# A 3x3 convolution with a second transform: columns as well as rows, and a running sum that lives in the output

## The chip, the cores and the metric

The kernel runs on one core of one Trainium2 chip. The metric is the device time of one execution in microseconds (us). A core has five engines that run side by side and meet through semaphores: PE (TensorE, matrix products), DVE (VectorE), ACT (ScalarE), POOL (GpSimd, here an issuer of DMAs) and SP (SyncE, an issuer of DMAs). PE's weight loads are listed apart as PEld. All DMAs run on the same 16 DMA engines.

## The reference

Four layers work on an input of 4 images x 256 channels x 64 x 64 pixels, fp32. Each adds to its input a function of the group-normalised input. Only the last one is changed; the others deliver its input in three pieces.

```
x = x + attention(gn(x))        # layer 0
x = x + ternary_conv(gn(x))     # layer 1
x = x + binary_block(gn(x))     # layer 2
x = x + conv3x3(gn(x), W) + bias  # layer 3: 256 -> 256 channels, 3x3, padding 1
...
W = weight * a / (1 + exp(weight * b))   # built from 64 x 64 x 3 x 3 and 16 pairs a, b
gn(v): mean and variance over 8 channels x 64 x 64 pixels of one image
```

## The kernel before, in words

The 256 channels are two tiles of 128 partitions, named t as an input (0 or 1) and co as an output. An image has 4096 pixels, which layer 3 handles in two halves h of 32 rows. A chunk is one image b, one half h and one output tile co: 16 chunks in all.

**The transform of layer 3.** The convolution's 3 rows of taps are replaced by a transform over rows (Winograd F(4,3)): six input rows give six transformed rows v[k], and six products m[k] give four output rows. Columns are plain: each v[k] is multiplied by three weight matrices, one for each dx, on windows of 64 columns shifted by dx. So a chunk has 6 (k) x 2 (t) x 3 (dx) = 36 products of 128x128 weights with 8 x 64 = 512 columns, all fp32 (line 1078). The weights are made in layer 0's score stage by the generator `weights_3`, a few DVE instructions at each step, and wait in DRAM (`u3_d`).

**`conv_layer`** holds layer 3. `prepare(b, t)` calls `load_3`: it loads x2 (layer 2's input), z and, for t=0, y (layer 2's output) and sums them in SBUF with scales that batch normalisation gave (`sg`, `sy2`): lines 1748, 1755 and 1758. The halves of the sum have six fixed buffers x0 to x5, by the table `X_PLACES`. Statistics come from `bn_stats` on DVE (line 1126), for the very first tile from ACT squares (line 1761). `norm` turns them into a scale and a shift, with small matmuls (lines 115 to 128). `transform(b, t, h)` writes the normalised half with ACT into a padded buffer (lines 1194 and 1198) and calls `input_rows`, 12 DVE instructions (lines 1052 to 1065), into one of six buffers t0 to t5. `chunk` calls `output_rows`: the products, two ACT copies (line 1096), 14 DVE instructions (lines 1098 to 1113), of which the last four add the result onto the sum in SBUF. `finish_3` stores that to `out` with one DMA of 1 MB from POOL (line 1772).

**Order.** `rest()` gives the program order; a list scheduler of the framework places the instructions of each engine by priority and expected time, and each engine then runs its own list strictly in that order. `high_priority` and `keep_in_program_order` override it in places. Products go into a ring of seven PSUM banks. For the first chunk, all products of t=1 are issued ahead of those of t=0 (`order = (1, 0)`), so that PE can begin before t=0 is ready.

**The border.** Layer 2 ends with convolutions of image 3. Its buffers and layer 3's share SBUF: a pool of layer 3 lies over what layer 2 has there, and each of its tiles waits until that is read. Of the sum, x and z are ready early; the scale `sy2` of y needs the statistics of all of layer 2.

Of the kernel before, what the change touches and what calls it, by code (L numbers as in the profile page):

```python
# [9 lines left out]
F32 = mybir.dt.float32  # L10
# [8 lines left out]
P = 128  # L19
B = 4  # L20
# [21 lines left out]
def network(ctx: ExitStack, tc, x, wqkv, relm, relt, relw, relv, counts, masks, vecs, rowv, ab, w1, l2w1, l2w2, l3w, mats, out):  # L42
# [25 lines left out]
    u3_d = scratch("u3_d", [P, 2, 3, 6, C])  # L68
    bk_d = [dram.tile([P, 2, 3, 4 * 3 * 64], BF16, name=f"bk_d{i}", tag=f"bk_d{i}") for i in range(2)]
# [339 lines left out]
    with ExitStack() as ph:  # L409
# [161 lines left out]

        def weights_2(i, g):
# [28 lines left out]
        def weight_steps():  # L601
            for t in range(2):
                for dx in range(3):
                    yield from weights_3(t, dx)
                    yield
            for i in range(2):
                for g in range(2):
                    yield from weights_2(i, g)
                    yield
# [137 lines left out]
    def from_scores(general, keep):  # L747
# [300 lines left out]
        def input_rows(v, pad, pinned):  # L1048

            d = [pad[:, r : r + 29 : 4, :] for r in range(6)]  # L1050
            stt = nc.vector.scalar_tensor_tensor
            start = stt(v[:, 5], d[2], -4.0, d[4], ALU.mult, ALU.add)
            if pinned:
                tc.keep_in_program_order(start)
            stt(v[:, 0], d[1], -4.0, d[3], ALU.mult, ALU.add)
            nc.vector.tensor_tensor(v[:, 1], v[:, 5], v[:, 0], ALU.add)  # L1056
            nc.vector.tensor_tensor(v[:, 2], v[:, 5], v[:, 0], ALU.subtract)
            nc.vector.tensor_tensor(v[:, 5], d[4], d[2], ALU.subtract)
            nc.vector.tensor_tensor(v[:, 0], d[3], d[1], ALU.subtract)
            stt(v[:, 3], v[:, 0], 2.0, v[:, 5], ALU.mult, ALU.add)  # L1060
            stt(v[:, 4], v[:, 0], -2.0, v[:, 5], ALU.mult, ALU.add)
            stt(v[:, 0], d[0], 4.0, d[4], ALU.mult, ALU.add)
            stt(v[:, 0], d[2], -5.0, v[:, 0], ALU.mult, ALU.add)
            stt(v[:, 5], d[1], 4.0, d[5], ALU.mult, ALU.add)
            stt(v[:, 5], d[3], -5.0, v[:, 5], ALU.mult, ALU.add)

        def output_rows(ring, taken, op, u, vs, co, xh, bias, name, order):


            ms = [None] * 6  # L1070
            c, sm = [None, None], [None, None]

            def product(k, t, first, last):
                if first:
                    ms[k] = ring[taken[0] % len(ring)].tile([P, 8, 64], F32, name=f"{name}_{k}", tag="conv")
                    taken[0] += 1
                for dx in range(3):
                    nc.tensor.matmul(  # L1078
                        ms[k], lhsT=u[t][:, dx, k, bass.ts(co, P)], rhs=vs[t][:, k, :, dx : dx + 64],
                        start=(first and dx == 0), stop=(last and dx == 2),  # L1080
                    )

            if order:
                for k in range(6):
                    product(k, order[0], True, False)
            for k in range(6):
                if order:
                    product(k, order[1], False, True)
                else:
                    product(k, 0, True, False)  # L1090
                    product(k, 1, False, True)
                if k in (2, 4):
                    i = k // 2 - 1
                    c[i] = op.tile([P, 8, 64], F32, name=f"{name}_c{i}", tag=f"c{i}", bufs=1)
                    sm[i] = op.tile([P, 8, 64], F32, name=f"{name}_s{i}", tag=f"s{i}", bufs=1)
                    nc.scalar.copy(c[i], ms[k])  # L1096
                    if i == 0:
                        nc.vector.scalar_tensor_tensor(sm[i], ms[1], bias, c[i], ALU.add, ALU.add)
                        nc.vector.scalar_tensor_tensor(c[i], ms[1], bias, c[i], ALU.add, ALU.subtract)
                    else:  # L1100
                        nc.vector.tensor_tensor(sm[i], ms[3], c[i], ALU.add)
                        nc.vector.tensor_tensor(c[i], ms[3], c[i], ALU.subtract)
            x4 = xh.rearrange("p (q r w) -> p q r w", r=4, w=64)
            (d12, d34), (s12, s34) = c, sm
            o = [op.tile([P, 8, 64], F32, name=f"{name}_o{r}", tag="o", bufs=1 if general else 2) for r in range(4)]
            nc.vector.tensor_tensor(o[0], ms[0], s12, ALU.add)
            nc.vector.tensor_tensor(o[0], o[0], s34, ALU.add)
            nc.vector.scalar_tensor_tensor(o[1], d34, 2.0, d12, ALU.mult, ALU.add)
            nc.vector.scalar_tensor_tensor(o[2], s34, 4.0, s12, ALU.mult, ALU.add)
            nc.vector.scalar_tensor_tensor(o[3], d34, 8.0, d12, ALU.mult, ALU.add)  # L1110
            nc.vector.tensor_tensor(o[3], ms[5], o[3], ALU.add)
            for r in range(4):
                nc.vector.tensor_tensor(x4[:, :, r, :], x4[:, :, r, :], o[r], ALU.add)
# [16 lines left out]
        X_PLACES = [(0, 1, 2, 3), (4, 5, 0, 2), (1, 3, 4, 0), (5, 2, 1, 4)]  # L1130

        def conv_layer(name, ph, weights, layout, own, load, biases, first, finish):
# [3 lines left out]
            ps_ = {k: pool(ph, f"{name}_{k}", 2 if k in ("a", "o") else 1) for k in layout.split()}  # L1136
            ap_, op, sp = ps_["a"], ps_["o"], ps_["s"]
            pst = pool(ph, f"{name}_pst", 1, PSUM)
            ring = [pool(ph, f"{name}_ps", 7, PSUM)]
# [3 lines left out]
            u = [ps_[f"u{t}"].tile([P, 3, 6, C], F32, name=f"{name}_u{t}", tag="u") for t in range(2)]  # L1143

            def set_up():
                for h in range(2):
                    nc.vector.memset(pads[h][:, 33 * h, :], 0.0)
                    nc.vector.memset(pads[h][:, 1 - h : 34 - h, 0], 0.0)
                    nc.vector.memset(pads[h][:, 1 - h : 34 - h, 65], 0.0)

            def load_weights(t, eng):
                for dx in range(3):
                    eng.dma_start(out=u[t][:, dx], in_=weights[:, t, dx])

            xs, vs, mvs, shifts = {}, {}, {}, {}

            def place(b, t):
                xs[b, t] = []
                for h in range(2):
                    s = X_PLACES[b][2 * t + h]  # L1160
                    xs[b, t].append(ps_[f"x{s}"].tile([P, HW // 2], F32, name=f"{name}x_{b}_{t}_{h}", tag="x"))
                return xs[b, t]

            def prepare(b, t):
                if t == 0 or b not in mvs:
                    mvs[b] = small(sp, [P, 2, 2])
                st = sp.tile([P, NB, 6], F32, name=f"{name}st_{b}_{t}", tag=f"st{t}")
                shifts[b, t], done = load(b, t, place(b, t), ap_, st, mvs[b][:, t, :], sp, pst, pads[0])
                if not done:
                    nc.vector.bn_aggr(mvs[b][:, t, :], st.rearrange("p k s -> p (k s)"))  # L1170
                if shifts[b, t] is not None:
                    nc.vector.tensor_tensor(mvs[b][:, t, 0:1], mvs[b][:, t, 0:1], shifts[b, t], ALU.add)

            norms = {}

            def norm(b, ts):
                gm, rs = norm_stats(sp, pst, mvs[b], ts, own, name)
                for t in range(ts.start, ts.stop):
                    i = t - ts.start
                    nb = small(sp, [P, 1])  # L1180
                    if shifts[b, t] is None:
                        nc.vector.scalar_tensor_tensor(
                            nb, gm[:, i : i + 1], -1.0, rs[:, i : i + 1], ALU.mult, ALU.mult
                        )
                    else:
                        nc.vector.tensor_tensor(nb, shifts[b, t], gm[:, i : i + 1], ALU.subtract)
                        nc.vector.tensor_tensor(nb, nb, rs[:, i : i + 1], ALU.mult)
                    norms[b, t] = nb, rs[:, i : i + 1]

            def transform(b, t, h, pinned=False):  # L1190

                nb, rs = norms[b, t]
                own_, other = xs[b, t][h], xs[b, t][1 - h]
                nc.scalar.activation(
                    pads[h][:, 1:33, 1:65], own_.rearrange("p (h w) -> p h w", w=64), AF.Identity, bias=nb, scale=rs
                )
                row_, dst = (other[:, 0:64], 33) if h == 0 else (other[:, HW // 2 - 64 : HW // 2], 0)
                nc.scalar.activation(pads[h][:, dst, 1:65], row_, AF.Identity, bias=nb, scale=rs)
                s = 2 * ((2 * b + h) % 3) + t
                v = ps_[f"t{s}"].tile([P, 6, 8, 66], F32, name=f"{name}tr_{b}_{t}_{h}", tag="tr")  # L1200
                input_rows(v, pads[h], pinned)
# [12 lines left out]
            def rest():  # L1214
                for b in range(B):
                    chunk(b, 0, 0, first if b == 0 else None)
                    if b + 1 < B:
                        prepare(b + 1, 0)
# [690 lines left out]
```

## Time and profile before

| | us |
|---|---|
| three runs | 2726.46, 2732.78, 2739.72 |
| median | 2732.78 |
| the profiled execution, own time | 2720.99 |
| span in its profile | 2719.2 |
| PE busy | 2391.5 (88%) |
| DVE busy | 1976.9 (73%) |
| ACT busy | 1204.6 (44%) |
| POOL busy | 104.7 (4%) |
| line 1078, the products of layer 3 | 503.7 |

The span runs from the first to the last instruction of the profiled execution; its own time is 1.8 us longer. Busy shares are averages over stages with different limits, so what matters for layer 3 is its own stage, the last 540 us. An idle time in a row stands before the group's own instructions, with what ended it.

### The profile page before, as it was taken

Reading aid. Unit: us, or ns where it says so; the run is one execution under the profiler, and the core shown is the slowest. Engines: PE = TensorE matmul, PEld = TensorE weight load, DVE = VectorE, ACT = ScalarE, POOL = GpSimd, SP = SyncE. Lnnn points to the kernel's source line nnn. Section 1 sums busy time; section 2 is a strip of 40 time slices with the busy share of each in tenths; the row PEclk is TensorE's granted clock in tenths of the full one; section 3 lists DMA queues with packets and bytes.
Section 4 is the critical chain, followed back from the end, with each engine's and each line's share of the span. In section 5 each row is a group of like instructions: output and inputs, shape, how many; then the busy total and the mean of one; then the engine's idle time right before and its main releaser. Section 6 shows DMA issues by size and latency. Waiting matters only on the chain. (4 is left out here: it accounts for less than half of the span.)

```text
span 2719.2 us, 78126 instructions
## 1 busy us (share of the span) xinstructions
PE 2391.5 (88%) x34632; PEld 1578.0 (58%) x34632; DVE 1976.9 (73%) x3370; ACT 1204.6 (44%) x1986; POOL 104.7 (4%) x201
## 2 busy tenths in 40 slices
PE   7999888888997788889775999998979869999998
PEld 4666655656665666667664777775545424444443
DVE  6766789888765465666668989887888877867742
ACT  4556355555555544454445666553458311110100
POOL 0000100000001000000000000000000000000000
PEclk9999899999999898988986999999989979999999
DMA  6866466666666877777777656424347742424110
GB/s 240 259 195 196 129 192 172 167 171 183 154 149 164 263 265 239 262 239 255 254 230 268 205 165 200 163 94 163 127 156 256 270 155 102 145 93 139 47 47 32
DMA packets 287996, 489.87 MB, mean 180 GB/s; under 512 B 32736, under 2 KB 149088, under 8 KB 274848
## 3 DMA queue, kind: packets, MB, share of 16 engines
q1 hardware_dynamic: 224992, 359.52, 43.5%
q0 software_dynamic: 14400, 66.53, 6.3%
q10 hardware_dynamic: 48256, 58.73, 6.3%
q8 instruction: 273, 4.47, 0.7%
q14 instruction: 75, 0.61, 0.1%
HBM read 281.46 MB, written 203.23 MB: 178 GB/s over the span
## 5 line engine op out<-in xcount | busy, mean ns | idle before, releaser
L1078 PE MATMUL gc<-gtr,g_u 128*128 128x512 f32 x1152 | 503.7, 599 | 12.0 <-DVE gtr L1056 6.7
L1078 PEld LDWEIGHTS gc<-gtr,g_u 128*128 128x128 f32 x1152 | 220.1, 192 | 287.5 <-issue 269.4
L515 DVE STREAM_TRANSPOSE t<-pd 128x1024 f32<-128x1024 f32 x256 | 304.4, 1228 | 86.1 <-PE pd L508 85.2
L508 PE MATMUL pd<-rm,qb 64*32 64x256 f32 x8192 | 307.2, 392 | 41.4 <-DVE t L515 32.3
L1469 PE MATMUL pc<-e_tr,e_k 128*64 128x512 bf16 x2304 | 264.8, 391 | 18.8 <-DVE e_tr L1458 11.7
L535 ACT ACTIVATE o<-pq 128x512 f32<-128x512 f32 x256 | 150.2, 592 | 270.2 <-PE pq L529 265.9
L1365 PE MATMUL dc<-dh,d_u 128*128 128x512 f32 x768 | 230.5, 411 | 20.9 <-ACT dh L1342 20.2
L508 PEld LDWEIGHTS pd<-rm,qb 64*32 64x32 f32 x8192 | 170.8, 109 | 133.2 <-DVE t L515 58.9
L919 ACT ACTIVATE pt<-pt,sm 128x512 f32<-128x512 f32 x256 | 162.3, 709 | 174.8 <-DVE pt L889 174.8
L1365 PE MATMUL dc<-dl,d_u 128*128 128x512 f32 x768 | 227.5, 407 | 2.5 <-DVE dl L1343 2.4
L1469 PEld LDWEIGHTS <-e_k 128*64 128x64 bf16 x2304 | 147.1, 113 | 133.4 <-issue 26.6
L529 PEld LDWEIGHTS pq<-t,t 64*64 64x64 f32 x8192 | 144.5, 137 | 84.7 <-issue 73.5
L529 PE MATMUL pq<-t,t 64*64 64x64 f32 x8192 | 166.9, 224 | 26.7 <-issue 22.2
L1365 PEld LDWEIGHTS dc<-dh,d_u 128*128 128x128 f32 x768 | 146.9, 193 | 61.4 <-ACT dh L1342 21.6
L1096 ACT COPY gc_c<-gc 128x512 f32<-128x512 f32 x32 | 18.6, 580 | 344.3 <-PE gc L1078 344.3
L1365 PEld LDWEIGHTS dc<-dl,d_u 128*128 128x128 f32 x768 | 145.6, 191 | 43.6 <-DVE dl L1343 5.2
L889 DVE TENSOR_TENSOR pt<-e_False,si_False 128x1024 f32<-128x1024 f32 x123 | 145.7, 1215 | 26.9 <-PE e_False L877 26.7
L877 PE MATMUL e_False<-qc_False,rw 32*128 32x256 f32 x984 | 128.4, 481 | 28.1 <-DVE pt L889 13.0
L541 ACT ACTIVATE sq<-o 128x1024 bf16<-128x1024 f32 x128 | 135.3, 1057 | 3.9
L291 PE MATMUL po<-xg,wt 128*128 128x512 f32 x256 | 120.3, 610 | 7.6 <-DVE st L298 6.0
L982 PE MATMUL pe_False<-pt,ve 128*32 128x64 f32 x4096 | 91.1, 243 | 36.9 <-issue 31.3
L957 PE MATMUL pa_False<-pt,vb 128*32 128x64 f32 x4096 | 100.0, 242 | 25.1 <-DVE o_False L966 18.1
(404 smaller groups left out, 3645.9 us busy)
## 6 DMA issues: line engine op xcount, KB each, us to landing
si_False<-qk_d SPq DMA_DIRECT2D x64, 1024.0 KB
qk_d<-o SPq DMA_DIRECT2D x496, 128.0 KB
x<-x_d SPq DMA_DIRECT2D x32, 1056.0 KB
xa<-in_x SPq DMA_DIRECT2D x16, 1024.0 KB
vt_d<-vs ACTq DMA_DIRECT2D x32, 512.0 KB
q_d<-qs SPq DMA_DIRECT2D x64, 256.0 KB
qb<-q_d SPq DMA_DIRECT2D x128, 128.0 KB
qc_False<-q_d SPq DMA_DIRECT2D x64, 256.0 KB
```

Source lines behind the costliest of these rows:

```text
L291: nc.tensor.matmul(psf, lhsT=wt[:, t, bass.ts(o, P)], rhs=xg[:, t, :], start=(t == 0), stop=(t == 1))
L508: nc.tensor.matmul(pds[t][32 * c : 32 * c + 32, m].rearrange("p j k -> p (j k)"), lhsT=q[rows, 2 * (gp % 2) + g, a, 32 * nb : 32 * nb + 32 ...
L515: nc.vector.transpose(ts[t][:, :, 32 * jh : 32 * jh + 32].rearrange("p a j b -> p j a b"), pds[t].rearrange("p m j k -> p j m k"),)
L529: nc.tensor.matmul(ps[nb][64 * g : 64 * g + 64, m, :], lhsT=ts[1][rows, n // 2, :, n % 2], rhs=ts[0][rows, n // 2, :, n % 2], start=True, ...
L535: nc.scalar.activation(o[:, :, n : n + 8, :], ps[nb].rearrange("p n (a b) -> p a n b", b=2), AF.Copy, accum_out=acc[:, nb, gp, col : col + 1],
L541: nc.scalar.activation(junk, part, AF.Square, accum_out=acc[:, 2, gp, col : col + 1])
L877: nc.tensor.matmul(rows_of_e[x_][:, :, :, par], lhsT=rw[rows, 63 - i : 127 - i].rearrange("p j r -> p (j r)"), rhs=q[rows, :, par, k % 2, ...
L889: nc.vector.tensor_tensor(dst, e, src, ALU.add)
L919: nc.scalar.activation(s, s, AF.Exp, scale=s2q[:, gp : gp + 1])
L1078: nc.tensor.matmul(ms[k], lhsT=u[t][:, dx, k, bass.ts(co, P)], rhs=vs[t][:, k, :, dx : dx + 64], start=(first and dx == 0), stop=(last and ...
L1365: nc.tensor.matmul(at[k], lhsT=u[t][:, dx, k, bass.ts(co, P)], rhs=v[:, k, :, dx : dx + 64], start=(first and p_ == 0 and dx == 0), stop=( ...
L1469: nc.tensor.matmul(m[64 * g : 64 * g + 64], lhsT=parts[:, g, i, k, dx, :], rhs=vs[g][:, k, 8 * (q % 2) : 8 * (q % 2) + 8, dx : dx + 64], s ...
```

## The change

- **Columns.** Products of even k (0, 2, 4) get a second transform over columns (Winograd F(2,3)): `input_columns` makes from four shifted column sets, with a step of two elements, four sets of 32 columns, and four weight matrices replace three. Each is a product with 8 x 32 = 256 columns. Two of the four share a PSUM bank as its halves. Odd k stay as they were. A chunk has 18 products of 512 columns and 24 of 256.
- **Weights.** `weights_c` makes the two mixed column weights from `u3_d` and stores them in `uc_d`. `load_weights` takes six DMAs for each t.
- **Output.** `columns` (two ACT half copies and one DVE sum from PSUM) and `whole` (one DVE sum that interleaves the columns) undo the column transform. The sum is not added on DVE: the result `o4` is added onto `out` in DRAM by a POOL DMA with `accum_op`. Only image 3's h=1 adds on DVE and stores from SP, in two parts. `o4` has one buffer.
- **Inputs.** `load_3` sums pieces of 512 pixels in rings: x five deep, z four, y three. Each sum is stored to `out` from ACT's queue; its statistics come from DVE's accumulated sum and an ACT square. `fetch` reads 33 rows back from `out` (POOL queue) for `transform`. Image 0's first half stays in SBUF, its x and z are asked for early, and its y comes as one DMA into the place of the t=0 weights.
- **Buffers and order.** Transformed inputs have four places for six; t=1 goes ahead with seven of the nine tiles; loads of the next image are held until a transform is done (`issue_after`). Layer 2's y tiles get a pool for each image.

```diff
+        def weights_c(t):
+            nc.gpsimd.dma_start(out=a, in_=u3_d[:, t, 0, 0:6:2])
+            nc.gpsimd.dma_start(out=c, in_=u3_d[:, t, 2, 0:6:2])
+            nc.gpsimd.dma_start(out=u[:, 3:6], in_=u3_d[:, t, 1, 0:6:2])
...
+            pinned(v.tensor_tensor(c, a, c, ALU.add))
+            v.tensor_scalar(c, c, 0.5, None, ALU.mult)
+            pinned(v.scalar_tensor_tensor(u[:, 0:3], u[:, 3:6], 0.5, c, ALU.mult, ALU.add))
+            v.scalar_tensor_tensor(u[:, 3:6], u[:, 3:6], -0.5, c, ALU.mult, ALU.add)
+            nc.gpsimd.dma_start(out=uc_d[:, t].rearrange("p c k o -> p (c k) o"), in_=u)
...
+        def input_columns(w, v):
+            f = v.rearrange("p k q w -> p (k q) w")
+            d = [f[:, :, r : r + 63 : 2] for r in range(4)]
+            for c, (i, j, op) in enumerate(
+                ((0, 2, ALU.subtract), (1, 2, ALU.add), (2, 1, ALU.subtract), (3, 1, ALU.subtract))
+            ):
+                last = nc.vector.tensor_tensor(w[:, c].rearrange("p k q w -> p (k q) w"), d[i], d[j], op)
+            return last
+
+        TILES = [(1, None), (2, (1, 2)), (2, (0, 3)), (3, None), (4, (1, 2)), (4, (0, 3)), (0, (1, 2)), (0, (0, 3)), (5, None)]
...
+                    for a, c in enumerate(cs):
+                        nc.tensor.matmul(
+                            m[:, a], lhsT=u2[:, c, k // 2, bass.ts(co, P)],
+                            rhs=v2[:, c, k // 2].rearrange("p q w -> p (q w)"), start=first and a == 0, stop=last and a == 1,
+                        )
...
+            def columns(i, copied, scratch_):
+                pair = halves(flat(ms[i]))
+                c2 = halves(copied)
+                nc.scalar.copy(c2[:, 0], pair[:, 1])
+                nc.scalar.mul(c2[:, 1], pair[:, 1], -1.0)
+                sd = halves(scratch_)
+                nc.vector.tensor_tensor(sd, pair[:, 0:1].to_broadcast([P, 2, 256]), c2, ALU.add)
+                return sd
+
+            def whole(i, sd, dst):
+                nc.vector.tensor_tensor(
+                    dst.rearrange("p (n a) -> p a n", a=2), halves(flat(ms[i])), sd, ALU.add
+                )
...
+            if res is None:
+                nc.gpsimd.dma_start(out=out_, in_=of, accum_op=ALU.add)
+            else:
+                for half in range(2):
+                    cols = bass.ts(half, HW // 4)
+                    nc.vector.tensor_tensor(of[:, cols], of[:, cols], res[:, cols], ALU.add)
+                    nc.sync.dma_start(out=out_[:, cols], in_=of[:, cols])
...
+            ps_ = {k: pool(ph, f"{name}_{k}", {"x": 5, "z": 4, "y": 3}.get(k, 1)) for k in layout.split()}
...
+            def fetch(b, t, h):
+                raws[b, t, h] = raw(b, t)
+                nc.gpsimd.dma_start(
+                    out=raws[b, t, h].rearrange("p q w -> p (q w)"),
+                    in_=out[b, bass.ts(t, P), 31 * h * 64 : (31 * h + 33) * 64],
+                )
...
                     chunk(b, 0, 0, first if b == 0 else None)
-                    if b + 1 < B:
-                        prepare(b + 1, 0)
+                    if more:
+                        with tc.issue_after(ready[b, 0, 0]):
+                            prepare(b + 1, 1)
                     chunk(b, 0, 1, None)
-                    if b + 1 < B:
-                        prepare(b + 1, 1)
+                    if more:
+                        with tc.issue_after(ready[b, 0, 1]):
+                            prepare(b + 1, 0)
                         norm(b + 1, slice(0, 2))
+                        for t in range(2):
+                            fetch(b + 1, t, 0)
                     chunk(b, 1, 0, None)
-                    if b + 1 < B:
+                    if more:
                         for t in range(2):
                             transform(b + 1, t, 0)
+                            fetch(b + 1, t, 1)
...
-            yp = pool(ph, "e_y")
+            yps = {b: pool(ph, f"e_y{b}") for b in (3, 0, 1, 2)}
...
+                    nc.scalar.activation(a, xt, AF.Square, accum_out=st[:, k, 1:2])
+                    if raw is None or k > 3:
+                        nc.scalar.dma_start(out=dst[:, bass.ts(k, HW // 8)], in_=xt)
...
+                if later:
+                    with tc.issue_after(loaded[0]):
+                        nc.sync.dma_start(out=y0, in_=y_d[0])
```

## The prediction

> **What bounds the kernel now.** I read the page's groups first, then stages, then time lines of PE and DVE across the border of the last two layers. The change touches only the last convolution, from about 2130 us, so that stage decides.
>
> ```profile
> L1078 PE MATMUL gc<-gtr,g_u 128*128 128x512 f32 x1152 | 503.7, 599 | 12.0 <-DVE gtr L1056 6.7
> L1078 PEld LDWEIGHTS gc<-gtr,g_u 128*128 128x128 f32 x1152 | 220.1, 192 | 287.5 <-issue 269.4
> ```
>
> One fp32 product is two MATMULs: 36 products in each of 16 chunks give 576, and the row counts 1152. The same stage by images (columns: length, busy PE, PEld, DVE, ACT, POOL with counts, clock, DMA share, GB/s):
>
> ```profile
> 2178.00:2223.00 45.00, 21.21 (x43) 9.38 (x43) 28.93 (x84) 9.71 (x22) 0.00 (x0) 0.73 0.66 216
> 2223.00:2345.00 122.00, 122.00 (x283) 54.18 (x284) 101.97 (x179) 17.03 (x19) 2.14 (x4) 0.98 0.27 95
> 2345.00:2467.00 122.00, 122.00 (x290) 54.31 (x289) 91.24 (x162) 14.49 (x17) 2.13 (x4) 1.00 0.34 116
> 2467.00:2590.00 123.00, 123.00 (x292) 54.70 (x291) 89.22 (x159) 14.48 (x17) 2.13 (x4) 1.00 0.26 93
> ```
>
> PE is busy all of every image and DVE three quarters of it: **PE bounds the convolution**. Its step is read from the ACT copies that repeat in each chunk, 30.90 us apart (72 MATMULs of 0.429):
>
> ```profile
> 2670.58 0.58 ACT L1096 COPY gc_c<-gc 128x512 f32<-128x512 f32 x1 [9.71 <-PE gc L1078]
> ...
> 2701.48 0.58 ACT L1096 COPY gc_c<-gc 128x512 f32<-128x512 f32 x1 [9.71 <-PE gc L1078]
> ```
>
> Ahead of it lies a hole. PE has the t=1 half of the first chunk from 2178.8, then waits for t=0, whose inputs wait for DMAs that were issued late:
>
> ```profile
> 2209.71 0.58 PE L115 MATMUL pst<-sm,mt 128*128 128x1 f32 x2 [16.33 <-DVE sm L1172]
> ...
> 2222.96 67.48 PE L1078 MATMUL gc<-gtr,g_u 128*128 128x512 f32 x151 [6.68 <-DVE gtr L1056]
> ```
> ```profile
> 2194.73 1.42 DVE L1748 SCALAR_TENSOR_TENSOR gx<-x,sg,gx 128x512 f32<-128x512 f32 x2 [5.37 <-DMA gx<-x_d]
> ...
> 2200.54 0.75 DVE L1758 SCALAR_TENSOR_TENSOR gx<-yq,sm,gx 128x512 f32<-128x512 f32 x1 [3.06 <-DMA yq<-y_d]
> ```
>
> PE ends near 2706.0, the span at 2719.2: a tail of 13.2 us (last sums, a POOL store, its landing).
>
> **What the Trainium skill says.** TensorE: Matmul & The Clock Gate, Back-to-back issue gap: N/2.4 + 2.5 ns once warm. The 0.429 agrees with two passes of 512 plus 2.5, so I price 256 columns at 0.216; this is an estimate from both. Its Step-by-step section says the next weights load during the running matmul; the trace has loads of 0.192, and they fit under 0.216. SBUF — State Buffer, Door 1 (the cacheline note): fp32 keeps full rate while two accesses hit each 16-byte line, which a step of two elements does; no run here shows such a DVE row. DMA: Bandwidth & Descriptors, SWDGE vs HWDGE vs iDMA: accumulating DMAs are issued by GpSimd only. The page gives no rate for them; the trace has none.
>
> **PE products: -81.** A new chunk has three whole tiles (k=1, 3, 5: 36 MATMULs of 512) and six half tiles (48 MATMULs of 256): 36 x 0.429 + 48 x 0.216 = 25.8 us, 5.1 less; over 16 chunks 81. Bounds: the closest row, `pv` (128x256, line 306), counts 120.0/512 = 0.234, beside 120.3/256 = 0.470 for `po` (line 291) there: again half. Taking 0.236 costs 16 us more over all chunks; I see no reason for less than 0.213.
>
> **The hole: -19 in time, but less work in it.** All x and z pieces of image 0 and y are now requested before layer 2 ends, into `r1`, `x`, `z`, `r0` and `u0`, which lie over `y0` to `y2` and the `e_x` ring. The last of these is read by the store of `z_d` that POOL issues at 2118.9, so they are free some 4 us later. DVE knows `sy2` at 2187 (2185 without the 2.6 us of DMA wait inside). Then: 8 sums at 0.67 = 5.3; last square 0.8; statistics and norm, 9.4 in the trace from L1117 to L1187 among other work, I take 7; pad 2.1; three operations until the first product, 1.9. That gives 2202. The t=0 weights share `u0` with y, so their 2.75 MB start only after the last square, near 2191.5; at the 10.0 us to landing that the DMA view gives for weight pieces, plus something for six at once, 2204. I take 2204 for the restart, against 2223. Before it PE does seven t=1 tiles, 9.5 us of work in place of 15.4. Bounds: 2198 to 2212.
>
> **DVE: +10 per image.** Single rows overlap, so I price DVE from start to start (first column start, second duration):
>
> ```profile
> 2223.43 0.75 DVE L1755 SCALAR_TENSOR_TENSOR gx<-yq,sm,gx 128x512 f32<-128x512 f32 x1
> 2224.10 0.70 DVE L1058 TENSOR_TENSOR gtr<-g_pad 128x528 f32<-128x528 f32 x1
> 2224.72 0.70 DVE L1059 TENSOR_TENSOR gtr<-g_pad 128x528 f32<-128x528 f32 x1
> ```
>
> A load sum costs 0.67, 528 elements 0.62, and 512 elements 0.60 in the same way (L1107 at 2269.29, L1108 at 2269.89). An image of before has 90 busy. Removed: 16 bn_stats, -9.6, and two aggregates, -0.7. Output: 16 operations in place of 14 in each of four chunks, +4.8 (`columns` and `whole` add six, the four residual adds go). `input_columns`: four of 768 elements, estimated 0.87 each, times four transforms: +13.9. Sum statistics: +1. Total about 100. If both strided kinds ran at half rate, another 19; less than 0.80 for 768 elements I exclude, since no such fp32 row here beats one element per 1.04 ns. PE needs 4 x 25.8 = 103 per image. **So DVE becomes 97% full during images 0 to 2**, where it was 74%; image 3 has no loads or next transforms and stays with PE.
>
> DVE runs in order, and it will not be 97% efficient: an x piece waits for the store of the fifth before it, a z piece for the square of the fourth. Four z pieces per about 5 us (landing, sum, square) is 1.25 us each, against 0.66 of DVE work. I charge 6 us per image, 18 in all. The first image is worse: after the restart DVE has 11 + 22 of transforms, 40 of outputs, 19 of loads and 22 of next transforms until chunk 5, 114 us from 2201, while PE arrives at 2307: +7.
>
> **Other moved or added work.** ACT: 16 squares (13 us), 24 half copies (9), 16 store issues (5), against 8 whole copies (4.6) now; 17 busy becomes about 40 of 103. SP: x goes in 64 pieces for 16, y in 25 for 32; its waits are those charged above; the last two chunks' stores move here. ACT's queue gets about 58 stores of the sum, POOL's loses 16 stores and gets 14 accumulates, 14 fetches, 12 weight loads (six now), and 8 for `weights_c`, early. Queued behind a waiting fetch is an accumulate, which holds the only `o4`; behind that are DVE and then PSUM. The cover: the last write of `o4` and the next chunk's first lie 17.2 us of PE apart (tiles 0 to 5), while a plain 1 MB store lands in 4.1. Bounds of an accumulate: 4.1, and four times that, 16: nothing in both, once the queue is free. DMA bytes rise from 14 MB per image to 23 (27 if accumulates count twice), 210 to 250 GB/s; the trace sustains 273 at 2050-2150. `weights_c`: 2 x 3.1 us of DVE at 0.87 and 0.48 in the score stage, 70 to 90% full; 0 to +6, I take 1. The tail loses a store of 1 MB and two adds: -4 (0 to -6). The separate `y` pools cost nothing; they only ease placement.
>
> **Sum.** 2204 + (16 x 25.8 - 9.5) = 2607; +4 for cold clock and small gaps (as 2223 + 479 became 2706); +9 tail: 2620, if PE alone decides. +18 + 7 for DVE, +1: **2646**, 73 below 2719.2. The profiled execution took 2720.99 and the median of the runs shown is 2732.78, 12 more; the same distance gives **2659**.
>
> **Rivals.**
> 1. PE stays the bound: DVE's slack is found by moving loads between windows. Now DVE runs without a gap from 2220 to 2254 when it has a backlog. 2620, median 2633.
> 2. DVE clearly bounds: strided rows at half rate or piece waits; 120 to 125 per image, 3 x 20 + 7: 2687, median 2700. The 52 us of DVE waits for `x_d` speak for it.
> 3. Half products don't halve: weight loads become the limit at 0.29 or more; 16 x 48 x 0.074 = 57, median 2716. The `pv` row speaks against it.
> 4. **Slower:** POOL's queue. If an accumulate (with the fetch ahead of it) needs more than 17.2 us, each of 14 chunks waits for `o4`. From 2659, it is slower than now from 74/14 = 5.3 more, a landing of 22.5 us; at 30 us it is 2659 + 14 x 12.8 = 2838. Nothing prices an accumulate here; 4.1 for the plain store speaks against.
>
> **Chances.** Forecast 0.55, rival 1 0.17, rival 2 0.13, rival 3 0.06, rival 4 0.09. 0.5%, some 14 us, is about what a measurement can tell. Faster 0.87, same 0.05 (edges of 2 to 4), slower 0.08. Range 2620 to 2715: rival 1 to the upper ends of 2 and 3.
>
> **What would show it.** Right: 128x256 rows near 0.216 step; PE restarts near 2204; chunk step 25.8 in image 3 and 27 to 28 before; DVE over 90% in images 0 to 2. Wrong: `o4` writes waiting for DMA; PE idle beside idle DVE; a restart after 2212; strided DVE rows above 1.2 us.

## The result, and the profile after

The changed kernel takes 2720.49 us (median, 2712.34 to 2735.55), the kernel before 2733.19 beside it: a ratio of **0.9961, 95% interval 0.9943 to 0.9979**. That is 12.7 us gained, within 0.5%, where 74 were forecast; 2720 lies above the range. The profiled execution took 2718.1 us, its span 2716.3.

The products did become cheaper. The groups of the page for the new line of whole tiles (512 columns) and of half tiles (256):

```profile
L1114 PE MATMUL gc<-gtr,g_u 128*128 128x512 f32 x576 | 265.1, 614 | 29.9 <-DVE gc_c L1169 13.4
L1121 PE MATMUL gc<-gtc,g_u 128*128 128x256 f32 x768 | 181.3, 391 | 4.2 <-DVE gc_o L1180 4.2
```

Together 446.4 us busy in place of 503.7. Where PE is not held up, two chunks begin 25.81 us apart (timeline of PE: start, duration):

```profile
2346.68 10.46 PE L1114 MATMUL gc<-gtr,g_u 128*128 128x512 f32 x24
...
2372.49 10.46 PE L1114 MATMUL gc<-gtr,g_u 128*128 128x512 f32 x24
```

But the stage did not shorten: from the restart with t=0 to PE's last product it took 483.6 us before (2222.96 to 2706.6) and takes 480.4 now (2226.38 to 2706.8), although 16 x 25.8 less the 9.5 done ahead is 403.3. **77 us are lost on PE.** PE is busy for 425.8 of the 480.4: it stands still for 54.6 us. The other 22 are some 4 of small matmuls for the norms, and products that take longer than at the step above (the granted clock is 0.93 over the stage). The same timeline across image 0 and image 1:

```profile
2226.38 5.39 PE L1114 MATMUL gc<-gtr,g_u 128*128 128x512 f32 x8 [10.07 <-DMA g_u<-u_d]
...
2313.11 0.59 PE L116 MATMUL pst<-sm,mt 128*128 128x2 f32 x2 [13.63 <-DVE sm L1253]
...
2408.22 8.36 PE L1114 MATMUL gc<-gtr,g_u 128*128 128x512 f32 x12 [4.60 <-DVE gc_c L1169]
...
2437.38 0.59 PE L116 MATMUL pst<-sm,mt 128*128 128x2 f32 x2 [11.34 <-DVE sm L1253]
```

L116 is the small matmul of the next image's group norm. It stands in PE's order amid the products and waits for statistics, so the products behind it wait too; the twelve after the 4.60 take 8.36 us in place of 5.31 at full clock. Two stretches of one image, then the image periods from one L116 to the next (columns: length, busy PE, PEld, DVE, ACT, POOL with counts, clock, DMA share, GB/s):

```profile
2340.00:2396.00 56.00, 56.00 (x190) 35.71 (x189) 53.92 (x91) 11.05 (x27) 1.85 (x3) 1.00 0.32 81
2396.00:2441.00 45.00, 29.06 (x80) 16.59 (x79) 25.15 (x67) 8.88 (x26) 1.83 (x3) 0.82 0.95 302
...
2313.11:2437.38 124.27, 108.33 (x335) 65.84 (x335) 102.25 (x197) 27.13 (x59) 5.63 (x8) 0.93 0.64 187
2437.38:2562.78 125.40, 108.99 (x341) 66.49 (x341) 102.47 (x197) 27.78 (x61) 5.66 (x8) 0.92 0.62 184
```

In the first stretch DVE is full with transforms and the DMA engines are two thirds idle. In the second the DMA engines are 95% busy, PE is idle for a third of the time and DVE for nearly half. An image takes 124 to 125 us; DVE has 102 of work in it, PE 103. Where DVE's list has the first sum for the next image, and what DVE does in the second stretch (its timeline):

```profile
2381.64 0.75 DVE L1869 SCALAR_TENSOR_TENSOR gx<-gz,sg,gx 128x512 f32<-128x512 f32 x1
...
2406.67 0.75 DVE L1869 SCALAR_TENSOR_TENSOR gx<-gz,sg,gx 128x512 f32<-128x512 f32 x1 [9.24 <-DMA gx<-x_d]
...
2430.52 0.75 DVE L1839 SCALAR_TENSOR_TENSOR gx<-yq,sm,gx 128x512 f32<-128x512 f32 x1 [6.07 <-DMA yq<-y_d]
```

The first sum comes 68.5 us after the L116 at 2313.11, behind all four transforms of image 1. Later DVE waits in order for an x piece and a y piece, with outputs of chunks queued behind. And why the pieces are late is seen in SP's own waits (total us, times, longest) from 2215 to 2600:

```profile
SPq L1865 <- ACT gz L1844: 182.1, 16, 64.8
SPq L1863 <- DMA out<-gx: 66.0, 33, 6.6
```

SP asks for a ring full of z pieces and then stands up to 64.8 us, until DVE, at last past its transforms, sums the first piece and ACT squares it. From then on everything is wanted at once.

**Which theory?** A: the loads of an image are squeezed into one burst; the DMA engines set its length, and DVE and PE wait in order. B: DVE's own throughput is the limit. C: the place of L116 in PE's order is.

### The profile page after: what moved, and what is told of

It reads as the page before. It is cut to its first block, busy times and chain, and to the rows that moved or that the text cites. A ratio compares the mean times of both kernels' runs of the same rounds, so it can differ in the third digit from the quotient of the medians.

```text
span 2716.3 us, 79190 instructions
## 1 busy us (share of the span) xinstructions
PE 2329.3 (86%) x34824; PEld 1620.0 (60%) x34824; DVE 2036.1 (75%) x3506; ACT 1250.4 (46%) x2148; POOL 127.4 (5%) x227
## 4 chain that ended last, share of the span: by engine, by line
PE 28%; DVE 15%; DMA 13%; ACT 4%; issue 4%; SPq 0%; POOL 0%; ACTq 0%; DVEq 0%; POOLq 0%
PE dc L1450 9%; PE gc L1114 4%; PE gc L1121 3%; DMA at_d<-o_False 3%; DMA x<-x_d 2%; PE den_False L952 2%; DMA gx<-x_d 2%; PE e_False L899 2%; PE pc L1554 2%; PE pr_False L970 2%; DVE pt L911 2%; PE pe_False L1004 1%; DVE gtc L1096 1%; DMA qc_False<-q_d 1%; PE pa_False L979 1%
## 5 line engine op out<-in xcount | busy, mean ns | idle before, releaser
L1114 PE MATMUL gc<-gtr,g_u 128*128 128x512 f32 x576 | 265.1, 614 | 29.9 <-DVE gc_c L1169 13.4
L1114 PEld LDWEIGHTS gc<-gtr,g_u 128*128 128x128 f32 x576 | 112.5, 197 | 161.6 <-issue 124.2
L530 PEld LDWEIGHTS pq<-t,t 64*64 64x64 f32 x8192 | 145.2, 138 | 83.8 <-issue 73.5
L1121 PE MATMUL gc<-gtc,g_u 128*128 128x256 f32 x768 | 181.3, 391 | 4.2 <-DVE gc_o L1180 4.2
L1121 PEld LDWEIGHTS gc<-gtc,g_u 128*128 128x128 f32 x768 | 149.9, 197 | 40.1 <-issue 13.9
```

What stands on the lines that cost most here:

```text
L530: nc.tensor.matmul(ps[nb][64 * g : 64 * g + 64, m, :], lhsT=ts[1][rows, n // 2, :, n % 2], rhs=ts[0][rows, n // 2, :, n % 2], start=True, ...
L1114: nc.tensor.matmul(ms[i], lhsT=u1[:, dx, k // 2, bass.ts(co, P)], rhs=v1[:, k // 2, :, dx : dx + 64], start=(first and dx == 0), stop=(las ...
L1121: nc.tensor.matmul(m[:, a], lhsT=u2[:, c, k // 2, bass.ts(co, P)], rhs=v2[:, c, k // 2].rearrange("p q w -> p (q w)"), start=first and a = ...
```

## The experiments

Gains below are against the changed kernel: 0.9961 less the experiment's ratio, times 2730 us. The ratio's interval is given each time. "Stage" is PE's time from the restart to its last product, with the part up to the L116 for image 1 and the rest. The last row is PE's products alone, at 0.429 and 0.216 each: 403.3, of which 58.5 stand ahead of the first L116 in the changed kernel's list (84 MATMULs of 512 columns, 104 of 256). In e5 that L116 stands some six half products later.

| run | stage | to first L116 | rest |
|---|---|---|---|
| changed kernel | 480.4 | 86.7 | 393.7 |
| e1 plain store | 463.9 | 83.8 | 380.2 |
| e2 no sum in out | 440.4 | 75.0 | 365.4 |
| e5 raw rows in place | 451.0 | 77.3 | 373.7 |
| e9 old columns | 441.0 | 86.9 | 354.1 |
| e12 e2 and e9 | 425.8 | 75.1 | 350.6 |
| PE alone | 403.3 | 58.5 | 344.8 |

**e1, the accumulate.**

```diff
-                nc.gpsimd.dma_start(out=out_, in_=of, accum_op=ALU.add)
+                nc.gpsimd.dma_start(out=out_, in_=of)
```

> The chunk results go to out by a plain store in place of the accumulating one, so the residual is left out of the output. Theory A (the loads of the next image are squeezed into one window of about 45 us in each image, in which the DMA engines are the limit, and DVE and PE wait in order behind them): the accumulates take part in that saturation (8.8 us to landing for 1 MB, against about 4 for a plain 1 MB store before); two of them fall into each burst, so each of three bursts gets 4 to 9 us shorter: 12 to 27 us faster than the changed kernel, about 2700. Theory B (DVE's own throughput is the limit): no change within 4 us. Theory C (the place of the norm matmul in PE's order is the limit, whatever the loads do): no change.

Measured: 0.9889 (0.9850 to 0.9929), a gain of 20 us, 16.5 of them in the stage. The rows of DMA issues (count, KB, median us to landing) for the changed kernel and for e1:

```profile
out<-gc_o POOLq DMA_DIRECT2D x14, 1024.0 KB, 8.8
```
```profile
out<-gc_o POOLq DMA_DIRECT2D x14, 1024.0 KB, 4.6
```

As A expected: the accumulates take part in the saturation. In the first period the DMA engines are busy for 65 us (0.56 of 116.06) in place of 79.5 (0.64 of 124.27), and the period is 8 us shorter. They hold nobody up by their own landing; writes of `o4` wait 0.5 us in all in the changed kernel.

**e2, the bytes.**

```diff
-                    if raw is None or k > 3:
+                    if b == 0 and (raw is None or k > 3):
...
-                    in_=out[b, bass.ts(t, P), 31 * h * 64 : (31 * h + 33) * 64],
+                    in_=(x2_d[b] if b else out[b])[bass.ts(t, P), 31 * h * 64 : (31 * h + 33) * 64],
```

with the plain store of e1.

> As e1, and for images 1 to 3 the sum is not stored to out, and the raw rows of the pads are fetched from x2 in place of out (same bytes); so the pads hold other data and the residual is left out. DVE, ACT and PE instructions stay the same. Bytes in a burst fall by 4 MB of stores and by the read side of accumulates, and no x piece waits for a store any more. Theory A: the stretch between full-speed PE windows shrinks from 45 us by some 15 us per image or more: 35 to 55 us faster than the changed kernel, about 2675. Theory B: at most 5 us faster. Theory C: at most 5 us faster.

Measured: 0.9806 (0.9769 to 0.9843), a gain of 42 us at the same instructions on PE, DVE and ACT, apart from DMA issues. The period falls to 110 to 111 us. DVE's *throughput* alone (B) is out. The number was right. DVE's list keeps its order, with the first sum behind four transforms. But e2 takes away two things, bytes and the x pieces' waits for stores, and doesn't tell them apart. The DMA engines lose 24.5 us of work in the first period (0.50 of 110.01 are 55.0), and the period loses 14.3: more than half of what is taken comes back, the rest ran beside DVE's work before.

**e3, the order.** `prepare(b + 2, 1)` before the second-half transforms of image b+1, `prepare(b + 1, 0)` right after the first chunk, no `issue_after`.

> The program order alone is changed: the first half of the next image's loads and sums is issued ahead of the second pair of transforms, one chunk earlier, the second half right after the first chunk, and the two gates that held them back are gone. Same instructions and bytes. Theory A: loads spread over two to three chunk windows instead of one and a half, so the DMA share falls below 0.9 and 20 to 45 us are gained against the changed kernel, about 2690. Theory B: DVE has the same work: no change within 5 us. Theory C: the norm matmul is where it was, but the statistics come earlier: as A. So this tells A and C from B.

Measured: 0.9928 (0.9901 to 0.9956), a gain of 9 us, below A's 20 to 45. For the statistics of images 1 to 3 PE now waits 6.35 at most, but it waits for DVE's `gc_s` of L1141 (up to 9.35), for image 0's statistics (9.68) and for a transform (8.80). A's size was wrong: DVE was still late. The interval overlaps that of the changed kernel.

**e4, the norm matmul.**

```diff
-                gm, rs = norm_stats(sp, pst, mvs[b], ts, own, name)
+                gm, rs = norm_stats(sp, pst, mvs[0], ts, own, name)
```

> The normalisation of images 1 to 3 uses the statistics of image 0, so neither PE's norm matmul nor the pads wait for the new statistics (that part of the computation is left out); all loads, sums and stores stay. Theory A: PE passes the norm matmul, but its chunk tiles then wait for DVE, which still waits in order for x and y pieces: 0 to 15 us faster than the changed kernel. Theory C: the 11 us of waiting and the cold clock after it go in each image: 30 to 45 us faster. Theory B: no change.

Measured: 0.9937 (0.9911 to 0.9962), a gain of 7 us; its interval overlaps that of the changed kernel, but C's 30 to 45 lie far outside it. PE passes L116 and then waits for DVE's outputs. Its waits from 2150 us on (total, times, longest):

```profile
PE gc L1114 <- DVE gc_c L1145: 24.9, 6, 8.4
PE gc L1114 <- DVE gc_c L1169: 14.5, 3, 7.3
```

C falls: L116 is only the first instruction in PE's order that meets a late DVE.

**e5, raw rows in place.**

```diff
-                if b == 0:
-                    raws[b, t, 0] = raw(b, t)
+                raws[b, t, 0] = raw(b, t)
...
-                        for t in range(2):
-                            fetch(b + 1, t, 0)
```

> For images 1 to 3 too, the sums of rows 0 to 31 are built in the raw tile itself, as image 0 does, so the upper raw rows are not fetched back from out (2 fetches of 1056 KB less per image) and four of eight x pieces do not pass through the ring of five, nor wait for its stores. Everything else, the accumulates included, stays. Theory A (each burst is limited by DMA bytes and by ring waits behind stores): the period of an image falls from 125 towards 115: 20 to 30 us faster than the changed kernel, about 2690. Theory B (DVE's throughput): no change within 5 us.

Measured: 0.9858 (0.9821 to 0.9896), a gain of 28 us with nothing left out; the period is 114.8 and 116.3. As A expected.

**e6, weights_c; e7, the first image's priorities.**

> weights_c is left out, and the two middle column weights are loaded from the row weights in its place (same bytes; the output is then not the convolution's). The score stage is then as before the change. Theory D (weights_c with its DMAs and its four DVE operations per half delays the score stage by the 10.9 us by which all later work is late): the first instruction of layer 2's last stage comes 8 to 11 us earlier and the kernel is 8 to 11 us faster than the changed kernel. Rival E (the 10.9 us are the spread of the score stage from run to run): 0 to 3 us, and the shift of that stage differs between profiles of the same program.

> Image 0's sums and its first transform lose their high priority, so DVE does them after layer 2's outputs in its order; the loads stay ahead. Theory F (the 12.7 us by which layer 2's last products are late come from those waits and operations placed amid layer 2's outputs): layer 2's last MATMUL comes 8 to 13 us earlier; the restart of the convolution with t=0 moves by less, since 12 us of transform then lie behind the end: 0 to 6 us faster than the changed kernel. Rival (the lateness is carried in from the score stage and from DMA alone): layer 2's last MATMUL stays within 3 us and the restart comes 5 to 12 us later.

e6: 0.9935 (0.9909 to 0.9960); 7 us, but its interval overlaps that of the changed kernel. All work after the score stage was 10.9 us later in the profile after than before (one row of layer 2 at 2091.50 and at 2102.40). In e6 that row comes at 2096.27, though its last products of the score stage begin at 870.48, as in the changed kernel (870.63). The same kernel profiled twice, as e5 and as e16, shows how far this place moves by itself:

```profile
863.30 2.12 PE L509 MATMUL pd<-rm,qb 64*32 64x256 f32 x64
```
```profile
879.94 1.96 PE L509 MATMUL pd<-rm,qb 64*32 64x256 f32 x64
```

16.6 us apart. So two single profiles can't price anything ahead of layer 2; D is not shown, and a cost of `weights_c` between 0 and 10 us stays open.

e7: 0.9959 (0.9942 to 0.9976), no gain. From that row of layer 2 to layer 2's last MATMUL it is 81.9 us before, 94.6 in the changed kernel and 85.5 in e7; but to PE's end it is 604.4 in the changed kernel and 607.8 in e7. So F is right on the cause for 9 of the 12.7 us, and its cure is none: the sums and the first transform take the place of layer 2's outputs on DVE, or come behind them, ahead of the restart.

**e8, the column transform undone**, with the new inputs kept: six whole tiles, three weights each.

> The column transform is undone (six whole row tiles of 512 columns, three weights each, as before the change), the new inputs by pieces, the sums in out, the fetches and the accumulates stay. PE then needs 30.9 us per chunk, 123.6 per image, and DVE 22 us per image less. Theory A: the same bytes now have 20 us more per image to move, so PE hardly waits between images: the convolution is near 16 x 30.9 after the restart, and the whole within 10 us of the changed kernel although PE has 81 us more work; 2715 to 2730. Rival G (PE's products were in truth the limit and got no shorter as a whole): 60 to 80 us slower than the changed kernel, near 2790.

Measured: 1.0085 (1.0054 to 1.0117), 34 us slower than the changed kernel and 23 slower than before. Between A's 10 and G's 60 to 80. Its windows for images 1 and 2, about a period each:

```profile
2308.00:2430.00 122.00, 121.70 (x281) 54.27 (x282) 75.36 (x158) 24.05 (x45) 5.67 (x8) 0.97 0.71 214
2430.00:2553.00 123.00, 123.00 (x293) 54.55 (x292) 74.68 (x155) 24.09 (x45) 5.68 (x8) 1.00 0.56 163
```

PE has no idle in them: with 75 us of DVE work in an image, the same loads hide. A is right there, though DVE's list is another too: its first sum of the next image comes after one transform, not four. What A missed is the start. In this layout SP asked for image 0's first x pieces only at 2190.21; PE waited 32.15 us for the first statistics, and the restart came at 2247. So it is no clean undo of one part. It shows one thing more: without those sums and the transform in it, layer 2's tail (measured in e7's way) took 69.7 us.

**e9, DVE's work.** `input_columns` for image 0 alone.

```diff
-                ready[b, t, h] = input_columns(v2, m).ins
+                ready[b, t, h] = (input_columns(v2, m) if b == 0 else last).ins
```

> input_columns runs for image 0 alone; images 1 to 3 use its column-transformed tiles again (so their half products are of old data), which takes 4 x 3.5 = 14 us of DVE from each of them. Loads, sums, stores, products stay. The question is what starts a burst. Theory A1 (the burst starts when DVE, behind with its transforms, reaches the first sum, and its length is set by the DMA engines): sums start some 7 us earlier in images 1 and 2 (two transforms) and the later transforms no longer push them, so the wait of PE falls by 7 to 14 us in each of two bursts, less in the first: 12 to 30 us faster than the changed kernel. Theory A2 (only the DMA engines count: the burst is as long as before whenever it starts, and starts with the program's gates): at most 5 us.

Measured: 0.9806 (0.9771 to 0.9840), a gain of 42 us, 39.4 of them in the stage. DVE's busy time in the stage falls from 377.7 to 338.3, some 13 us for each of three images. The gain is more than A1's 30, and against A2. The bytes are all there, so the DMA engines do not bound the image alone either. But this run is not the removal of work that it was meant to be. The order of DVE's list changed with it: the first sum for the next image comes 18.4 us after the L116 at 2318.20, behind one transform in place of four (A1 reckoned with 7 us earlier). From there on loads and transforms run side by side (its timeline of DVE, and a stretch of 20 us):

```profile
2336.58 0.74 DVE L1872 SCALAR_TENSOR_TENSOR gx<-gz,sg,gx 128x512 f32<-128x512 f32 x1
```
```profile
2338.00:2358.00 20.00, 20.00 (x67) 12.32 (x66) 20.00 (x38) 6.64 (x19) 0.54 (x1) 1.00 0.87 286
```

DVE and PE have no idle time in it, while the DMA engines are 87% busy. From 2215 to 2600 DVE's waits for x, z and y pieces fall to 22 us, from 51 in the changed kernel. So the bytes alone do not make the burst: **the loads go on when DVE's list reaches the first sum**, for SP resumes at 2383.18 in the changed kernel and at 2340.07 here. With all sums behind the transforms, DVE's work and part of the loading stand in series. How much of the 42 us is the order and how much the lesser work is not separated, and why the order changed is not shown (the edit also moves `ready`, the gate of the loads). e3, which brought some sums forward with all of DVE's work kept, gained 9; so the order alone was not enough there.

**e10 and e11, order and ring on e5.**

> e5 (raw rows 0 to 31 built in place), and the order of e3 in the form that the raw tiles allow: the next image's t=1 half is loaded and summed between the two second-half transforms, the t=0 half right after the first chunk, without gates. Theory A1: sums and loads are spread over more of the image; the period of e5, 115 to 116 us, falls towards 106 to 110, 10 to 25 us faster than e5, near 2675. Rival (e3 gained only 9 us because waits move to other DVE instructions in its order): within 5 us of e5.

> e10 with one buffer moved from the x ring to the z ring (x 4, z 5; four x pieces pass the ring in an image). If the z ring's wait for the squares (81 us of SP's waiting in e5) is what now holds the loads, 3 to 10 us faster than e10; if DMA bytes hold them, within 3 us.

Measured: 0.9919 (0.9897 to 0.9941) and 0.9921 (0.9893 to 0.9949), both about 17 us slower than e5. The gain of theory A1 is out, and the rival, within 5 us, was only nearer: in e10 the period stays 115.9 (2377.60 to 2493.48 between the same waits), and the restart is later, since sums of image 1 that wait for pieces (13.29 us for one) now stand between image 0's transforms; PE waits 18.48 us for the first of these. The deeper z ring of e11 gives nothing in this order.

**e12, both at once.** e2 and e9.

> e2 and e9 together: for images 1 to 3 no sum stores, raw rows fetched from x2, plain stores for accumulates, and the column-transformed tiles of image 0 used again (the output is not the convolution's). Theory S (DVE's work and its waits for pieces add up to the image's period, and PE's 103 us is the floor below them): together they go below the floor, PE runs from restart to end in 405 to 415 us, and the kernel lands 75 us below the changed one, near 2643; less than the 86 of the two gains added, since the floor cuts it. Rival (part of the stall is PE's or DVE's order around the norm matmul, independent of both): 8 us or more of PE waiting per image stay, and the kernel is at 2660 or above.

Measured: 0.9713 (0.9675 to 0.9751), a gain of 68 us; 84 would be the sum. Two stretches from its first L116 (2298.48), each as long as PE's four chunks, 103.2 us:

```profile
2298.48:2401.68 103.20, 102.94 (x331) 63.99 (x332) 93.47 (x198) 29.77 (x62) 4.81 (x9) 0.97 0.61 210
2401.68:2504.88 103.20, 103.20 (x342) 64.05 (x341) 88.81 (x180) 26.54 (x62) 4.27 (x8) 1.00 0.43 154
```

PE has next to no wait left in images 1 to 3: the rest takes 350.6 us, 6 over PE's products. So PE is the floor beneath, as theory S said. But the run can't show that the two gains add as in series: e9 alone is within 3.5 us of it there (354.1), and has the same new order of DVE's list. What e2 adds to e9 lies mostly in image 0 (86.9 becomes 75.1). The stage of 425.8 is above S's 405 to 415, and the kernel's median, 2655, lies between S's 2643 and the rival's 2660. What remains in image 0, some 17 us over its products, was not taken apart further (waits of 4.21 and 6.15 and a cold clock are seen in it).

**e13 and e14, column operations on POOL**, on e5: one and two of the four.

```diff
-                last = nc.vector.tensor_tensor(w[:, c]..., d[i], d[j], op)
+                eng = nc.gpsimd if c in (0, 1) else nc.vector
+                one = eng.tensor_tensor(w[:, c]..., d[i], d[j], op)
```

> e5, with one of the four column operations of each transform on POOL. DVE loses 4 x 0.87 = 3.5 us per image. Theory S: 2 to 4 us per image come back, 6 to 12 us faster than e5, near 2683. Rival (POOL's operation is slow, waits behind DMA issues in POOL's order, or takes access to SBUF from DVE, so that DVE waits for it before it overwrites the tile): same as e5 or slower by up to 15 us.

> As e13 with two of the four on POOL: DVE loses 7 us per image. Theory S: 4 to 7 us per image, 12 to 20 us faster than e5, near 2675. Rival: twice the loss of e13.

Measured: 0.9873 (0.9828 to 0.9917), not told apart from e5, and 0.9940 (0.9894 to 0.9985), some 22 us slower: the rival came true. Groups of e14 on POOL and on DVE, from 2220 to 2700 us:

```profile
L1098 POOL TENSOR_TENSOR gtc<-gtm 128x768 f32<-128x768 f32 x30 | 72.7, 2441 | 109.7 <-DVE gtm L1085 99.9 <-PE gc L1124 9.8
```
```profile
L1098 DVE TENSOR_TENSOR gtc<-gtm 128x768 f32<-128x768 f32 x30 | 42.9, 1472 | 0.0
```

The 30 operations left on DVE average 1472 ns; in e5 all 60 of that stretch are there, at 950:

```profile
L1096 DVE TENSOR_TENSOR gtc<-gtm 128x768 f32<-128x768 f32 x60 | 53.4, 950 | 0.0
```

The Trainium skill gives a reason (SBUF — State Buffer, Who interferes with whom): a DVE instruction with two inputs in SBUF and a GpSimd instruction that reads SBUF share a port, and one blocks the other. The rows agree, and so does another: L1177 on DVE, with two inputs in SBUF, took 1.39 us at 2380.73, while POOL was at work, for 0.68 elsewhere. An estimate for POOL from its 2.6 cycles an element at 1.2 GHz (GPSIMD Engine Reference, Elementwise — side-by-side cycle accounting) is 1.66 us; measured are 2.44 on average in e14, and a median of 4.40 in e13.

**e15 to e17, the z ring.** e5 with rings x 4, z 5 in place of 5 and 4, and both kernels again on one chip.

> e5 with one buffer moved from the x ring to the z ring (x 4, z 5), nothing else. If the ring of z pieces limits how early loads can be asked for, one more piece on the way in each round of four takes up to a quarter of the 12 us that an image of e5 is over PE's 103: 3 to 9 us faster than e5. If DVE's work and the bytes set the period, within 3 us of e5, near 2692.

> The kernel of e5 again, beside e17 on one chip: 0.986 of the kernel before, about 2690.

> The kernel of e15 again. If the z ring's depth is a limit of its own, 3 to 11 us faster than e16; if not, within 3 us.

e15: 0.9819 (0.9767 to 0.9871). Side by side: e16 2696.72 us (2694.83 to 2710.01), 0.9866 (0.9839 to 0.9893); e17 **2685.86** us (2675.39 to 2693.34), 0.9829 (0.9797 to 0.9862). No run of e17 is as slow as the fastest of e16: 11 us. The profiles say where: the image periods are 111.0 and 111.0 in e17 and 111.8 and 109.4 in e15, for 114.9 and 117.9 in e16. So in this order of DVE's list the depth of the z ring is a limit of its own; in e11's it was not. e17 leaves nothing out and is faster than both kernels: 46 us below the kernel before on that chip.

## Why the prediction was wrong, step by step

- **PE products, -81: right.** The chunk step is 25.81 where 25.8 was worked out; the half products do halve, so rival 3 is out. But the saving was counted as time on the path in every image, and there it wasn't: 77 us went into PE's waits (55), slower products (some 18, where 4 had been charged for cold clock and gaps) and small matmuls (4). Rival 1 is out with it.
- **DVE, +10 to about 100: right.** 102.3 and 102.5 are measured. `input_columns` was put at 0.87 per operation from start to start; four in a row take 3.56 us. The Trainium skill's cacheline note (SBUF — State Buffer, Door 1) is borne out: a step of two fp32 elements costs nothing extra here.
- **Piece waits, 6 us per image and 7 for the first: the step that failed.** Over PE's products alone, 28 us are lost up to the first L116, 23 in each of the two periods after it and 3 behind them: 77, where 18 and 7 for waits and 4 for cold clock make 29. The 6 came from a rate, four z pieces in 5 us, which by its own figures, 0.59 more per piece than DVE's work, gives 9 and not 6. It took for granted that the loads run all along the image beside DVE's work. In this kernel they can't: rings of 4 and 5 pieces fill early, then SP stands until DVE's list reaches the first sum, 68.5 us into the image. e2, with fewer bytes, comes to a period of 110, about what 103 and 6 forecast; e9, with earlier sums and less work, comes close to PE's own time. The 97% that the prediction worked out for DVE was a sign: an engine so full, with its loads released by its own progress, leaves little to hide a late load in. The 7 for the first image has a slip too: PE was to arrive at 2307, but with the 9.5 us done ahead, which the sum does take off, it is 2298, and the 7 becomes 17.
- **"DMA 210 to 250 GB/s; the trace sustains 273": the wrong average.** Over an image 187 is measured, but in the burst 302 at a share of 0.95. And the bytes are not alike: over 50 us of a burst the changed kernel moves 299 GB/s at 0.96 (from 2390), e1 with plain stores 354 at 0.98 (from 2380).
- **The hole, restart at 2204: 11.5 late.** 2226.38 less the 10.9 carried from the score stage is 2215.5. The term is when DVE knows `sy2`. The sum to 2202 runs from 2185 and not from the 2187 named beside it; measured is 2206.3 (the last reciprocal at 2206.13), less 10.9 is 2195.4, some 10 later. Asking for x and z early was put at no cost; their sums and the first transform lengthen layer 2's tail by 12.7 us (94.6 for 81.9; 85.5 in e7, 69.7 in e8, which have fewer of them there). Its rows show DVE waiting in order for image 0's pieces amid layer 2's outputs:

```profile
2143.48 0.75 DVE L1869 SCALAR_TENSOR_TENSOR gx<-gz,sg,gx 128x512 f32<-128x512 f32 x1 [5.41 <-DMA gz<-z_d]
...
2178.09 0.75 DVE L1869 SCALAR_TENSOR_TENSOR gx<-gz,sg,gx 128x512 f32<-128x512 f32 x1 [2.75 <-DMA gz<-z_d]
```

  From `sy2` on it is 20 us, where 19 were forecast, and the weights come last, as forecast. A gain of 7.5 is left of 19.
- **POOL's queue, accumulates, tail: right.** The landing of 8.8 lies between the bounds of 4.1 and 16 and below 17.2, so rival 4 is false. PE's end to the span's end is 9.5, for 12.6 before (PE's last product ends at 2706.6).
- **The +12 from span to median** held for the kernel before, whose profile had a short score stage (858.79 for its last products; those of the other profiles begin between 858 and 880). The changed kernel's profile lies 2.4 below its median. So 483.6 and 480.4 of the stage, and the medians, are what can be compared, not the two spans.

The terms add up to within 1 us: 2646, with 48 more lost in the stage than charged, 11.5 for the late restart and 10.9 carried in, is the span of 2716.

Rival 2 was nearest: 120 to 125 us per image, 2700. Its reason was half right (waits for pieces, no half rate), and the restart, 11.5 us late, makes over half of the rest.

## What to carry to other kernels

When one engine's progress releases the loads that it will wait for, through a short ring, charge nothing as hidden until a trace shows the two running side by side; look at them in windows of tens of microseconds, not per loop, and find where the first release stands in the engine's list. A run that takes work away tells its price only if the rest keeps its order: compare the lists as well as the times, above all where a scheduler places the instructions. And traffic that "nothing waits for", like an accumulate or a store of a running sum, is paid by the loads that share the burst with it.

## What the runs showed of the hardware that was not expected

- An accumulating DMA of 1 MB takes more of the DMA engines than a plain one. The rows of the POOL queue (packets, MB, share of 16 engines over the span), changed kernel and e1:

```profile
q0 software_dynamic: 17632, 84.29, 9.9%
```
```profile
q0 software_dynamic: 17632, 84.29, 8.3%
```

  The same packets and MB: 268.9 against 223.7 us of all engines, 3.2 us more for each of the 14 if the whole difference is theirs.
- PE pays for waits twice: after one of 4.60 us twelve products took 8.36 us in place of 5.31, and over the stage PE was busy for 425.8 us with products that take 403.3 at the full step.
- The score stage's end moves by up to 16.6 us between two profiled executions of one kernel, while the stage from the restart to PE's end differs by 3 (451.0 in e5 and 454.0 in e16, the same kernel).
